# Four graph-attention layers: the four-head output computed transposed, with elu taken from PSUM

## The chip, the cores and the metric

The kernel runs on one core of one Trainium2 chip. The metric is the device time of one execution in microseconds (us), as the median of several runs; lower is better. In profile lines PE is the matrix engine (PEld its weight loads), DVE the vector engine, ACT the scalar engine, POOL the GpSimd engine and SP the queue that issues the transfers.

## What is computed

There are 128 independent graphs of 128 nodes with 512 features. Each passes through four attention layers; after each comes a residual and a layer norm. The change lies in layer 1, which has two attentions in a row. The first has four heads of 256 features:

```python
xl = (x @ W).reshape(B, N, H, F)                       # H = 4, F = 256
e = leaky_relu(asrc[:, :, None, :] + adst[:, None, :, :], 0.2)
attn = softmax(where(mask[..., None], e, -1e9), axis=1)
out = einsum('bsdh,bshf->bdhf', attn, xl).reshape(B, N, H * F) + bias
h = elu(out)                                           # 1024 features
```

Then `h` is multiplied by W2 (1024 to 512 features) and goes through the second attention, of one head. As the weights of one output node sum to one, a bias that is added to every node's features adds the same bias to the output.

## The kernel before

A graph's 128 nodes lie on the 128 partitions, and a graph stays on chip through all layers. All data is float32; each float32 multiply of the matrix engine is two records (two MATMUL with their weight loads) in the profile, a transpose one.

`graph(g)` is a generator that emits one graph's work and stops at each `yield`; we call the part between two yields a step. The outer loop passes over all graphs in flight, oldest first, and lets each emit one step; a new graph joins every 10 passes (`STAGGER`). So in the steady state a pass emits steps r, r+10, r+20 and so on, of graphs that are ten passes apart, and ten passes emit the work of one graph. The tile framework then fixes each engine's queue: it follows the order of emission by priority, but may put a ready instruction ahead of one that waits. Each engine works its queue in order.

`attend` is one softmax: POOL multiplies the identity by the destination scores (`dg`, L160), PE spreads them over the partitions (`pd`, L167), ACT adds the source score (L177), DVE does leaky relu (L181) and adds the mask with a running minimum (L187), ACT takes exp with row sums (L194), DVE inverts the sums (`ri`, L200), PE transposes the weights (`pp`, L203) and DVE copies them to SBUF (`pt`, L206). A graph does this six times: `l0` (one head), `l1` (four), `l2` (one), `l30` and `l31` (four each, the two halves of layer 2's eight heads) and `l4` (one).

The first attention of layer 1 goes so. PE transposes `x1` (L234); `px` (L294) multiplies it by W1 in two halves of 512 columns, of which ACT copies the first to `xl` (L299) and DVE the second (L301). After `attend`, four multiplies `pa` (L311) take the weights `pt` of a head as the stationary operand and 256 columns of `xl` as the moving one. DVE scales by `ri` and adds the bias (L319), takes the minimum with zero (L324), ACT takes exp (L326), DVE forms elu (L328). PE transposes the 1024 features in eight blocks (`h1T`, L234), ACT and DVE copy them (L336, L338), and `pc` (L344, two columns for the scores) and `px` (L352, W2) use them as stationary operands.

PSUM has eight banks of 128 x 512 float32, taken in turn by every `bank()`.

Of the kernel before, what the change touches and what calls it, by code (L numbers as in the profile page):

```python
# [8 lines left out]
F32 = mybir.dt.float32  # L9
I32 = mybir.dt.int32  # L10
AF = mybir.ActivationFunctionType
ALU = mybir.AluOpType
AX = mybir.AxisListType

P = 128
SLOPE = 0.2
EPS = 1e-5
# A masked score is e - BIG, which rounds to -BIG for every e that a score can take.
BIG = float(2.0**100)
FMAX = 3.0e38  # L20
# A graph starts when the one before it has taken this many of its steps.
STAGGER = 10


# [1 line left out]
def tile_gat_stack(  # L26
# [19 lines left out]
    w_attn: bass.AP,  # L46
    out: bass.AP,
):
    """Four graph-attention layers with residual and layer norm. Each graph has 128 nodes, one
    per partition, and passes through all layers on chip; several graphs are in flight."""  # L50
    nc = tc.nc
    B, N, F = x.shape
    H1, FH = a1_src.shape
    HF = H1 * FH
    H2, FO = ah1.shape
    KF = F // P
    KH = HF // P
# [6 lines left out]
    def bank(name):  # L64
        return psum.tile([P, 512], F32, tag="ps", name=name)

# [1 line left out]
    ident = const.tile([P, P], F32, name="ident")  # L68
    make_identity(nc, ident)
    ones = const.tile([P, P], F32, name="ones")  # L70
# [5 lines left out]
    neghalf = const.tile([P, 1], F32, name="neghalf")  # L76
    nc.vector.memset(neghalf, -0.5)

# [1 line left out]
    def rows(ap, n, name, pool=const):  # L80
        t = pool.tile([P, n], F32, name=name)
        nc.scalar.dma_start(out=t, in_=ap.partition_broadcast(P))
# [5 lines left out]
    b1t = rows(b1, HF, "b1t")  # L88
# [6 lines left out]
    for h in range(H2):  # L95
        nc.scalar.dma_start(out=wht[:, :, h, :], in_=wh[h].rearrange("(k p) o -> p k o", p=P))

    # Scores are x @ (W @ a): the products of the weights come first, once.
    wc1 = const.tile([P, KF, 2 * H1], F32, name="wc1")
    wc2 = const.tile([P, KH, 2], F32, name="wc2")  # L100
    wc3 = const.tile([P, KF, 2 * H2], F32, name="wc3")
# [1 line left out]
    with tc.tile_pool(name="setup", bufs=1) as setup:  # L103
        for s, a in enumerate((a1_src, a1_dst)):
            at = rows(a.rearrange("h f -> (h f)"), HF, f"a1_{s}", setup)
            for k in range(KF):
                pr = setup.tile([P, H1, FH], F32, tag="pr1", name=f"pr1_{s}_{k}", bufs=2)
                nc.vector.tensor_mul(pr.rearrange("p h f -> p (h f)"), w1t[:, k, :], at)
                nc.vector.tensor_reduce(
                    out=wc1[:, k, s * H1 : (s + 1) * H1], in_=pr, op=ALU.add, axis=AX.X  # L110
                )
        for s, a in enumerate((a2_src, a2_dst)):
            at = rows(a.rearrange("h f -> (h f)"), F, f"a2_{s}", setup)
            for k in range(KH):
                pr = setup.tile([P, F], F32, tag="pr2", name=f"pr2_{s}_{k}", bufs=2)
                nc.vector.tensor_mul(pr, w2t[:, k, :], at)
                nc.vector.tensor_reduce(out=wc2[:, k, s : s + 1], in_=pr, op=ALU.add, axis=AX.X)
        for s, a in enumerate((ah1, ah2)):
            at = rows(a.rearrange("h f -> (h f)"), F, f"ah_{s}", setup)
            for k in range(KF):  # L120
                pr = setup.tile([P, H2, FO], F32, tag="pr3", name=f"pr3_{s}_{k}", bufs=2)
                nc.vector.tensor_mul(
                    pr.rearrange("p h f -> p (h f)"), wht[:, k].rearrange("p h f -> p (h f)"), at
                )
                nc.vector.tensor_reduce(
                    out=wc3[:, k, s * H2 : (s + 1) * H2], in_=pr, op=ALU.add, axis=AX.X
                )
        fc = setup.tile([OUT, F], F32, name="fc")
        nc.scalar.dma_start(out=fc, in_=w_fc)
        ac = setup.tile([OUT, 2], F32, name="ac")  # L130
        for s in range(2):
            nc.scalar.dma_start(
                out=ac[:, s : s + 1],
                in_=w_attn[0:1, s * OUT : (s + 1) * OUT].rearrange("u o -> o u"),
            )
        for s in range(2):
            # The same column for every output row: the product lands on all partitions.
            acb = setup.tile([OUT, P], F32, name=f"acb_{s}")
            nc.vector.tensor_copy(acb, ac[:, s : s + 1].to_broadcast([OUT, P]))
            pf = bank(f"pf_{s}")  # L140
            nc.tensor.matmul(pf, lhsT=acb, rhs=fc, start=True, stop=True)
            nc.vector.tensor_copy(wf[:, s, :], pf)

    io = ctx.enter_context(tc.tile_pool(name="io", bufs=3))
    wk = ctx.enter_context(tc.tile_pool(name="wk", bufs=3))
# [6 lines left out]
        nc.sync.dma_start(out=at, in_=adj[g])  # L152
        return xt, at

    def attend(g, lay, src, dst, mask, nh, res):
        """softmax over j of lrelu(src[i] + dst[j]) + mask[i, j], as (not normalised, transposed)
        weights [j, h, i] and the inverse of their sums [i, h], for each head."""
        n = f"{lay}_{g}"
        dg = wk.tile([P, 4, P], F32, tag="diag", name=f"dg_{n}")
        nc.gpsimd.tensor_mul(  # L160
# [37 lines left out]
        yield  # L198
        ri = sm.tile([P, 4], F32, tag="ri", name=f"ri_{n}")
        nc.vector.reciprocal(ri[:, :nh], rs[:, :nh])  # L200
        pp = bank(f"pp_{n}")
        for h in range(nh):
            nc.tensor.transpose(pp[:, h * P : (h + 1) * P], z[:, h, :], ident)  # L203
# [6 lines left out]
        res.append((pt, ri))  # L210

    def norm(y, n):
        """(y - mean) / sqrt(var + eps) over the features, in place."""
        st = sm.tile([P, 6], F32, tag="st", name=f"st_{n}")
        nc.vector.bn_stats(st, y)
        mv = sm.tile([P, 2], F32, tag="mv", name=f"mv_{n}")
        nc.vector.bn_aggr(mv, st)
        yield
        rd = sm.tile([P, 1], F32, tag="rd", name=f"rd_{n}")
        nc.gpsimd.tensor_scalar_add(rd, mv[:, 1:2], EPS)  # L220
        nc.gpsimd.tensor_tensor(out=rd, in0=rd, in1=neghalf, op=ALU.pow)  # L221
        yield
        nc.vector.tensor_scalar(  # L223
            out=y, in0=y, scalar1=mv[:, 0:1], scalar2=rd, op0=ALU.subtract, op1=ALU.mult
        )
        yield
# [9 lines left out]

    def graph(g, loaded):
        x0, adj_t = loaded
# [1 line left out]
        m3 = sm.tile([P, P], F32, tag="m3", name=f"m3_{g}", bufs=6)  # L240
        m2 = sm.tile([P, P], F32, tag="m2", name=f"m2_{g}", bufs=6)
        m1 = sm.tile([P, P], F32, tag="m1", name=f"m1_{g}", bufs=6)
# [5 lines left out]
                out=m, in0=a, scalar1=0.0, scalar2=-BIG, op0=op, op1=ALU.mult  # L248
            )

# [1 line left out]
        sc0 = sm.tile([P, 2], F32, tag="sc0", name=f"sc0_{g}")  # L252
        for s, (wv, init) in enumerate(((w0s, b0t), (w0d, 0.0))):
            jk = wk.tile([P, F], F32, tag="junk", name=f"jk0_{g}_{s}", bufs=2)
# [5 lines left out]
        res = []  # L260
# [11 lines left out]
        )  # L272
        yield from norm(x1, f"n0_{g}")

# [1 line left out]
        for xT, pb, _ in transposed(x1, KF, f"x1T_{g}", "xT"):  # L276
            yield
            nc.scalar.copy(xT.rearrange("p k i -> p (k i)"), pb)
# [12 lines left out]
        for c in range(2):  # L291
            px = bank(f"px1_{g}_{c}")
            for k in range(KF):
                nc.tensor.matmul(  # L294
                    px, lhsT=xT[:, k, :], rhs=w1t[:, k, c * 512 : (c + 1) * 512],
                    start=(k == 0), stop=(k == KF - 1),
                )
            if c == 0:
                nc.scalar.copy(xl[:, :512], px)  # L299
            else:  # L300
                nc.vector.tensor_copy(xl[:, 512:], px)  # L301
        yield
        yield from attend(g, "l1", sc1[:, H1:], sc1[:, :H1], m1, H1, res)
        pt, ri = res.pop()
        z1 = wk.tile([P, HF], F32, tag="z1", name=f"z1_{g}", bufs=2)
        t1 = wk.tile([P, HF], F32, tag="t1", name=f"t1_{g}", bufs=2)
        for c in range(2):
            pa = bank(f"pa1_{g}_{c}")
            for u in range(2):
                h = 2 * c + u  # L310
                nc.tensor.matmul(  # L311
                    pa[:, u * FH : (u + 1) * FH], lhsT=pt[:, h, :],
                    rhs=xl[:, h * FH : (h + 1) * FH], start=True, stop=True,
                )
            yield
            for u in range(2):
                h = 2 * c + u
                cols = slice(h * FH, (h + 1) * FH)
                nc.vector.scalar_tensor_tensor(  # L319
                    out=z1[:, cols], in0=pa[:, u * FH : (u + 1) * FH], scalar=ri[:, h : h + 1],  # L320
                    in1=b1t[:, cols], op0=ALU.mult, op1=ALU.add,
                )
        # elu(z) = max(z, exp(min(z, 0)) - 1)
        nc.vector.tensor_scalar_min(t1, z1, 0.0)  # L324
        yield
        nc.scalar.activation(t1, t1, AF.Exp)  # L326
        yield
        nc.vector.scalar_tensor_tensor(  # L328
            out=z1, in0=t1, scalar=-1.0, in1=z1, op0=ALU.add, op1=ALU.max
        )  # L330
        yield
        for hT, pb, c in transposed(z1, KH, f"h1T_{g}", "hT"):
            yield
            dst = hT[:, 4 * c : 4 * c + 4, :].rearrange("p k i -> p (k i)")
            if c == 0:
                nc.scalar.copy(dst, pb)  # L336
            else:
                nc.vector.tensor_copy(dst, pb)  # L338
        yield

# [1 line left out]
        pc = bank(f"pc2_{g}")  # L342
        for k in range(KH):
            nc.tensor.matmul(  # L344
# [21 lines left out]
        )  # L366
        yield from norm(x2, f"n1_{g}")

# [1 line left out]
        for xT, pb, _ in transposed(x2, KF, f"x2T_{g}", "xT"):  # L370
            yield
            nc.scalar.copy(xT.rearrange("p k i -> p (k i)"), pb)
# [38 lines left out]
        nc.vector.tensor_add(x3, x3, x2)  # L411
        yield from norm(x3, f"n2_{g}")

# [1 line left out]
        sc4 = sm.tile([P, 2], F32, tag="sc4", name=f"sc4_{g}")  # L415
        for s in range(2):
            jk = wk.tile([P, F], F32, tag="junk", name=f"jk3_{g}_{s}", bufs=2)
# [21 lines left out]
        yield from norm(y, f"n3_{g}")  # L439
        nc.sync.dma_start(out=out[g], in_=y)  # L440

# [1 line left out]
    loads = {0: load(0)}  # L443
    active, nxt, tick = [], 0, 0
    while active or nxt < B:
# [42 lines left out]
```

## Time and profile before

| | |
|---|---|
| time, median of 3 runs | 4495.4 us (4493.48 to 4498.8) |
| span of the profiled execution | 4494.5 us (its own time is not recorded apart from its span) |
| busy: PE, DVE, ACT, POOL | 97%, 82%, 44%, 37% of the span |
| granted clock of the matrix engine | 0.995 |
| one graph in the steady state | 33.9 us between equal points of two cycles of the chain |

The profile page gives the busy time of each engine, the span in 40 slices, the transfers, and the chain of work that ended last. Two adjoining records of one engine overlap in it, so the spacing of the starts says more about the rate than the duration of a record. The trace behind it gives each instruction with its start, its duration, and what ended the idle time before it.

### The profile page before, as it was taken

The page shows a single profiled execution, that of the slowest core. Times are in us where ns is not written, and L with a number is a line of the kernel's source. Part 1 is how long each engine was busy: PE and PEld are TensorE (multiplying, and loading weights), DVE is VectorE, ACT ScalarE, POOL GpSimd, SP SyncE. Part 2 cuts the span into 40 slices and gives each one's busy share as a digit, 9 for nine tenths or more (in the row PEclk, how much of TensorE's full clock was granted, in tenths as well). Part 3 has the DMA queues.
Part 4 walks back from the last instruction along what each step waited for, and adds up shares of the span by engine and source line. Part 5 has one row for each costly group of instructions (what it writes and reads, how often), then busy time and mean ns, then how long its engine had stood idle before and what let it go on. Part 6 is the DMA issues. An engine that isn't in the chain of part 4 may idle for free.

```text
span 4494.5 us, 61235 instructions
## 1 busy us (share of the span) xinstructions
PE 4348.2 (97%) x18692; PEld 2640.8 (59%) x18692; DVE 3702.8 (82%) x11464; ACT 1968.8 (44%) x6785; POOL 1659.6 (37%) x2438
## 2 busy tenths in 40 slices
PE   1999999999999999999999999999999999999997
PEld 0565666666566666566566666656656656656664
DVE  5688888888888888888888888888888888888887
ACT  0344444444444444444444444444444444444443
POOL 1233333333333333333333333333333333333332
PEclk9999999999999999999999999999999999999998
DMA  2000000000000000000000000000000000000000
GB/s 92 10 17 18 18 19 17 20 19 17 20 19 17 19 20 17 19 20 17 19 17 19 18 19 19 17 20 19 17 19 19 17 19 20 17 19 20 16 10 15
DMA packets 63142, 88.16 MB, mean 20 GB/s; under 512 B 10816, under 2 KB 27200, under 8 KB 62816
## 3 DMA queue, kind: packets, MB, share of 16 engines
q1 hardware_dynamic: 55296, 75.52, 5.1%
q10 hardware_dynamic: 7520, 8.72, 0.6%
q8 instruction: 152, 2.49, 0.2%
q14 instruction: 174, 1.43, 0.1%
HBM read 50.66 MB, written 33.55 MB: 19 GB/s over the span
## 4 chain that ended last, share of the span: by engine, by line
PE 88%; DVE 10%; POOL 1%; ACTq 0%; issue 0%; ACT 0%; DMA 0%; POOLq 0%; SPq 0%; DVEq 0%
PE px L352 20%; PE px L294 20%; PE px L384 10%; PE pd_l L167 9%; PE pa L400 5%; PE pa L311 5%; PE pc L344 4%; DVE z_l L181 4%; PE pp_l L203 3%; PE pa L426 3%; PE pc L284 2%; PE pc L376 2%; DVE pt_l L206 2%; DVE z_l L187 2%; PE x1T_p L234 1%; PE x2T_p L234 1%
## 5 line engine op out<-in xcount | busy, mean ns | idle before, releaser
L160 POOL TENSOR_TENSOR dg_l<-ident,sc 128x128 f32<-128x128 f32 (+1 forms) x768 | 648.6, 845 | 1246.7 <-PE pa L311 585.5
L352 PE MATMUL px<-w2t,h1T 128*128 128x512 f32 x2048 | 941.7, 603 | 0.0
L194 ACT ACTIVATE z_l<-z_l,nm_l 128x128 f32<-128x128 f32 x1920 | 757.8, 414 | 413.3 <-DVE nm_l L187 413.1
L294 PE MATMUL px<-w1t,x1T 128*128 128x512 f32 x2048 | 913.5, 599 | 0.0
L177 ACT ACTIVATE z_l<-pd_l,sc 128x128 f32<-128x128 f32 x1920 | 565.5, 375 | 483.6 <-PE pd_l L167 408.3
L294 PEld LDWEIGHTS px<-w1t,x1T 128*128 128x128 f32 x2048 | 380.5, 191 | 430.5 <-issue 430.2
L352 PEld LDWEIGHTS px<-w2t,h1T 128*128 128x128 f32 x2048 | 369.7, 190 | 367.8 <-issue 367.8
L187 DVE CUSTOM_DVE_ANT_0 z_l<-z_l,m 128x128 f32<-128x128 f32 x1920 | 567.3, 337 | 8.8
L356 ACT COPY xl<-px 128x512 f32<-128x512 f32 x128 | 75.0, 586 | 1068.1 <-PE px L352 1068.1
L167 PE MATMUL pd_l<-dg_l,ones 128*128 128x512 f32 (+1 forms) x1536 | 515.8, 435 | 15.3 <-POOL dg_l L160 15.2
L223 DVE TENSOR_SCALAR x<-x,mv_n,rd_n 128x512 f32<-128x512 f32 x384 | 294.1, 766 | 277.1 <-POOL rd_n L221 277.1
L181 DVE SCALAR_TENSOR_TENSOR z_l<-z_l 128x128 f32<-128x128 f32 (+1 forms) x768 | 504.3, 657 | 8.3 <-ACT z_l L177 8.3
L384 PE MATMUL px<-wht,x2T 128*128 128x512 f32 x1024 | 471.0, 603 | 0.0
L247 POOL TENSOR_SCALAR m<-adj 128x128 f32<-128x128 int32 x256 | 256.0, 1000 | 560.3 <-DVE nm_l L187 549.3
L206 DVE COPY pt_l<-pp_l 128x128 f32<-128x128 f32 (+1 forms) x768 | 369.7, 481 | 90.0 <-PE pp_l L203 89.9
L194 ACT ACTIVATION_READ_ACCUMULATOR z_l<-z_l,nm_l 128x1 f32 x1920 | 399.6, 208 | 0.0
L203 PE MATMUL pp_l<-ident,z_l 128*128 128x128 f32 x1920 | 341.8, 275 | 13.0 <-ACT z_l L194 12.6
L400 PEld LDWEIGHTS pa<-xl,pt_l 128*128 128x128 f32 x2048 | 259.2, 192 | 151.0 <-DVE pt_l L206 91.7
L203 PEld LDWEIGHTS pp_l<-ident,z_l 128*128 128x128 f32 x1920 | 240.4, 145 | 180.3 <-issue 129.6
L221 POOL TENSOR_TENSOR rd_n<-rd_n,neghalf 128x1 f32<-128x1 f32 x512 | 306.9, 599 | 32.5
L167 PEld LDWEIGHTS pd_l<-dg_l,ones 128*128 128x128 f32 x1536 | 243.1, 192 | 124.7 <-issue 98.6
L301 DVE COPY xl<-px 128x512 f32<-128x512 f32 x128 | 88.6, 692 | 269.6 <-PE px L294 269.6
(83 smaller groups left out, 6694.3 us busy)
## 6 DMA issues: line engine op xcount, KB each, us to landing
x<-in_x_dram SPq DMA_DIRECT2D x128, 256.0 KB, 2.6
out_dram<-y SPq DMA_DIRECT2D x128, 256.0 KB, 2.0
adj<-in_adj_dram SPq DMA_DIRECT2D x128, 64.0 KB, 1.7
w1t<-in_L_gnn_W_dram ACTq DMA_DIRECT2D x1, 2048.0 KB, 10.9
w2t<-in_L_gnn_W_dram ACTq DMA_DIRECT2D x1, 2048.0 KB, 16.0
wht<-in_L_gnn_W_dram ACTq DMA_DIRECT2D x8, 128.0 KB, 5.4
b1t<-in_L_gnn_b_dram ACTq DMA_DIRECT2D x1, 512.0 KB, 6.1
a<-in_L_gnn_att_src_dram ACTq DMA_DIRECT2D x1, 512.0 KB, 4.3
```

What stands on the lines that cost most here:

```text
L160: nc.gpsimd.tensor_mul(dg[:, :nh, :], ident.unsqueeze(1).to_broadcast([P, nh, P]), dst.unsqueeze(2).to_broadcast([P, nh, P]),)
L167: nc.tensor.matmul(pd[:, : nh * P], lhsT=ones, rhs=dg[:, :nh, :].rearrange("p h j -> p (h j)"), start=True, stop=True,)
L177: nc.scalar.activation(z[:, h, :], pd[:, h * P : (h + 1) * P], AF.Identity, bias=src[:, h : h + 1])
L181: nc.vector.scalar_tensor_tensor(out=z[:, :nh, :], in0=z[:, :nh, :], scalar=SLOPE, in1=z[:, :nh, :], op0=ALU.mult, op1=ALU.max,)
L187: nc.vector.tensor_tensor_reduce(out=z[:, h, :], in0=z[:, h, :], in1=mask, scale=-1.0, scalar=FMAX, op0=ALU.add, op1=ALU.min, accum_out=nm ...
L194: nc.scalar.activation(z[:, h, :], z[:, h, :], AF.Exp, bias=nm[:, h : h + 1], scale=-1.0, accum_out=rs[:, h : h + 1],)
L203: nc.tensor.transpose(pp[:, h * P : (h + 1) * P], z[:, h, :], ident)
L206: nc.vector.tensor_copy(pt[:, :nh, :].rearrange("p h i -> p (h i)"), pp[:, : nh * P])
L294: nc.tensor.matmul(px, lhsT=xT[:, k, :], rhs=w1t[:, k, c * 512 : (c + 1) * 512], start=(k == 0), stop=(k == KF - 1),)
L352: nc.tensor.matmul(px, lhsT=hT[:, k, :], rhs=w2t[:, k, :], start=(k == 0), stop=(k == KH - 1))
L384: nc.tensor.matmul(px, lhsT=xT[:, k, :], rhs=wht[:, k].rearrange("p h o -> p (h o)"), start=(k == 0), stop=(k == KF - 1),)
L400: nc.tensor.matmul(pa[:, u * FO : (u + 1) * FO], lhsT=pt[:, u, :], rhs=xl3[:, h * FO : (h + 1) * FO], start=True, stop=True,)
```

## The change

In the first attention of layer 1 the output is computed with features on the partitions. Both halves of `px` are now taken out of PSUM by DVE with an addition of the bias. `attend` gets `scaled=True`: POOL multiplies the four heads' weights by the inverse sums before they are transposed, with a yield of its own behind it. The output multiplies take 128 columns of `xl` as the stationary operand and the transposed weights as the moving one: eight of 128 columns in place of four of 256. ACT reads each PSUM bank twice, with exp and with relu, and DVE forms min(exp(z) - 1, relu(z)) straight into `hT`. The eight transposes, the two copies behind them, the scaling out of PSUM and the minimum with zero go. Comments were removed too. From here on steps and lines are those of the kernel before, unless said otherwise.

```diff
-    def attend(g, lay, src, dst, mask, nh, res):
+    def attend(g, lay, src, dst, mask, nh, res, scaled=False):
...
         nc.vector.reciprocal(ri[:, :nh], rs[:, :nh])
+        if scaled:
+            nc.gpsimd.tensor_mul(
+                z[:, :nh, :], z[:, :nh, :], ri[:, :nh].unsqueeze(2).to_broadcast([P, nh, P])
+            )
+            yield
         pp = bank(f"pp_{n}")
...
-            if c == 0:
-                nc.scalar.copy(xl[:, :512], px)
-            else:
-                nc.vector.tensor_copy(xl[:, 512:], px)
-        yield
-        yield from attend(g, "l1", sc1[:, H1:], sc1[:, :H1], m1, H1, res)
+            cols = slice(c * 512, (c + 1) * 512)
+            nc.vector.tensor_add(xl[:, cols], px, b1t[:, cols])
+        yield
+        yield from attend(g, "l1", sc1[:, H1:], sc1[:, :H1], m1, H1, res, scaled=True)
         pt, ri = res.pop()
-        z1 = wk.tile([P, HF], F32, tag="z1", name=f"z1_{g}", bufs=2)
-        t1 = wk.tile([P, HF], F32, tag="t1", name=f"t1_{g}", bufs=2)
+        e1 = wk.tile([P, KH, P], F32, tag="e1", name=f"e1_{g}", bufs=2)
+        r1 = wk.tile([P, KH, P], F32, tag="r1", name=f"r1_{g}", bufs=2)
+        hT = wk.tile([P, KH, P], F32, tag="hT", name=f"hT_{g}", bufs=2)
         for c in range(2):
             pa = bank(f"pa1_{g}_{c}")
-            for u in range(2):
-                h = 2 * c + u
+            for u in range(4):
+                k = 4 * c + u
                 nc.tensor.matmul(
-                    pa[:, u * FH : (u + 1) * FH], lhsT=pt[:, h, :],
-                    rhs=xl[:, h * FH : (h + 1) * FH], start=True, stop=True,
+                    pa[:, u * P : (u + 1) * P], lhsT=xl[:, k * P : (k + 1) * P],
+                    rhs=pt[:, k * P // FH, :], start=True, stop=True,
                 )
             yield
-            for u in range(2):
-                h = 2 * c + u
-                cols = slice(h * FH, (h + 1) * FH)
-                nc.vector.scalar_tensor_tensor(
-                    out=z1[:, cols], in0=pa[:, u * FH : (u + 1) * FH], scalar=ri[:, h : h + 1],
-                    in1=b1t[:, cols], op0=ALU.mult, op1=ALU.add,
-                )
-        # elu(z) = max(z, exp(min(z, 0)) - 1)
-        nc.vector.tensor_scalar_min(t1, z1, 0.0)
-        yield
-        nc.scalar.activation(t1, t1, AF.Exp)
-        yield
-        nc.vector.scalar_tensor_tensor(
-            out=z1, in0=t1, scalar=-1.0, in1=z1, op0=ALU.add, op1=ALU.max
-        )
-        yield
-        for hT, pb, c in transposed(z1, KH, f"h1T_{g}", "hT"):
-            yield
-            dst = hT[:, 4 * c : 4 * c + 4, :].rearrange("p k i -> p (k i)")
-            if c == 0:
-                nc.scalar.copy(dst, pb)
-            else:
-                nc.vector.tensor_copy(dst, pb)
+            cols = slice(4 * c, 4 * c + 4)
+            nc.scalar.activation(e1[:, cols, :].rearrange("p k i -> p (k i)"), pa, AF.Exp)
+            nc.scalar.activation(r1[:, cols, :].rearrange("p k i -> p (k i)"), pa, AF.Relu)
+            yield
+            nc.vector.scalar_tensor_tensor(
+                out=hT[:, cols, :], in0=e1[:, cols, :], scalar=-1.0, in1=r1[:, cols, :],
+                op0=ALU.add, op1=ALU.min,
+            )
         yield
```

## The prediction

> **What bounds the kernel now.** First the page: engine totals and slices.
>
> ```profile
> PE 4348.2 (97%) x18692; PEld 2640.8 (59%) x18692; DVE 3702.8 (82%) x11464; ACT 1968.8 (44%) x6785; POOL 1659.6 (37%) x2438
> PE   1999999999999999999999999999999999999997
> DVE  5688888888888888888888888888888888888887
> PE 88%; DVE 10%; POOL 1%; ACTq 0%; issue 0%; ACT 0%; DMA 0%; POOLq 0%; SPq 0%; DVEq 0%
> ```
>
> PE is busy in every slice behind the start, and the last line, the shares of the chain that ended last, gives PE 88%. But 10% of it is DVE, so I read one cycle of the chain in order of time.
>
> ```profile
> 2002.70 0.79 PE pc L284 x8
> ...
> 2012.51 0.12 PE pp_l L203
> ...
> 2012.66 0.29 DVE pt_l L206
> 2012.95 0.62 DVE z_l L181
> ...
> 2014.53 0.86 DVE z_l L181
> 2015.39 0.61 DVE pt_l L206
> ...
> 2016.04 1.10 PE pa L400 x8
> ...
> 2027.54 0.84 PE pa L400 x8
> 2028.38 0.44 PE x2T_p L234 x4
> 2028.83 0.22 PE pd_l L167 x2
> 2029.05 0.87 PE pa L311 x4
> ...
> 2036.62 0.79 PE pc L284 x8
> ```
>
> A cycle (one graph) is 2036.62 - 2002.70 = 33.92 us. All is PE except 2012.66 to 2016.0, where the chain goes through DVE. What PE does meanwhile stands in its timeline:
>
> ```profile
> 2012.46 0.60 PE L234 MATMUL h1T_p<-ident,z 128*128 128x128 f32 x4
> 2012.89 0.60 PE L203 MATMUL pp_l<-ident,z_l 128*128 128x128 f32 x4
> 2013.33 1.02 PE L361 MATMUL pa<-xl,pt_l 128*128 128x512 f32 x2
> 2014.19 0.60 PE L234 MATMUL h1T_p<-ident,z 128*128 128x128 f32 x4
> ...
> 2015.60 0.27 PE L203 MATMUL pp_l<-ident,z_l 128*128 128x128 f32 x1
> 2016.04 1.10 PE L400 MATMUL pa<-xl,pt_l 128*128 128x64 f32 x8 [0.17 <-DVE pt_l L206]
> ```
>
> PE works there too, from 2012.51 to 2015.71 (2015.60 and one transpose of 0.11), then has nothing until 2016.04: 0.33 us lost. The L400 group then takes 0.94 to the next start (2016.98) where it takes 0.84 at 2027.54: 0.10 more. The stall is 0.43 a cycle; the other 33.49 is PE work without a gap. So PE's queue is the bound, with one joint where DVE sets the pace, and both groups of `h1T` transposes lie exactly at that joint.
>
> **PE, part by part, per graph.**
> Removed: eight `h1T` transposes at 0.44 per four (the x2T piece): -0.88.
> The output multiplies: before, eight records of 256 columns at 0.87 per four: 1.74. After, sixteen records of 128 columns, each with new weights. Columns alone give 0.87/4/2 = 0.109 each, as much per graph as before. Nearest rows: `pd_l` of 128 columns, 0.22 for two, 0.11 each; transposes, 0.44 for four, 0.11 each, also with new weights every time; L284, 8 columns, 0.79 for eight, 0.099, so a weight load alone costs about that and lies under the multiply. Ends: 16 x 0.107 = 1.71 (-0.03) and the stalled L400 group, 1.10 for eight, 0.1375 each, 2.20 (+0.46). I take 0.115 each, 1.84 (+0.10), near to the 0.11 rows.
> The Trainium skill, "TensorE: Matmul & The Clock Gate", section "Back-to-back issue gap", speaks against the split: in a stream of weight loads and multiplies the spacing is set by both, so narrower moving operands pay. Here 0.11 at 128 columns is what columns alone give; if load and stream added (0.099 + 0.107), the sixteen would cost 3.3, +1.6, and the change would lose.
>
> **The joint.** The saved 0.88 lies inside the window that DVE ends. If the joint stayed as it is, PE would come 0.88 earlier to L400 and wait 0.88 longer. Whether it stays is a matter of the order of emission. I counted yields: 79 steps before, 77 after (three fewer for elu and copies, one more for scaling), so everything behind comes two steps earlier against layers 0 and 1 of younger graphs. The DVE work of the window is `pt` of `l0`, leaky relu and mask of `l30` (0.62 and four at about 0.21), leaky relu of `l1` (0.86), and only then `pt` of `l31` (0.61), which L400 waits for. The leaky relu of `l30` falls there because its `pd` (step 46) is emitted two passes behind the 7 us `px` of L294 (step 14). After, it is step 44: same pass, older graph, ahead of that `px`. Its ACT and DVE work can run under the 7 us. The `pp` of `l31` moves from step 58 to 56 and its `pt` to 57, ahead of the leaky relu of `l1` (step 18). Between that `pp` and L400 PE then has L361 0.86, `pd` of `l1` 0.86 and two transposes 0.22: 1.94 for DVE to make one copy of 0.61. So the stall mostly goes: I take -0.30 of the 0.43, ends 0 and -0.43 for the forecast, +0.88 as a rival.
> What is late next: `pc` L344 needs the second elu half. Behind its multiplies stand ACT 0.63 and 0.59 (128x512 rows of L433 and L356) and DVE 0.69 (L435): 1.9 us. PE has 1.94 as above, then L400 0.84, `pp` of `l30` 0.44 and the first half of `pc` 0.79: 4.0. Covered by 2.1. The `pp` of `l1` waits for the new POOL step: ACT 4 x 0.375, DVE 0.76 + 4 x 0.42 (L187 with its accumulator read), ACT 4 x 0.62, DVE 0.16, POOL 1.29 make 7.9 us; in that time PE has two transposes, L400 and `pp` of `l30` (1.5), `pc` L344 (1.6), L352 (7.1), then `pm`, L266, L426, L400, x2T and `pd` of `l2` (3.3): 13.5. Covered by 5.6.
>
> **The other engines.** DVE, page means: out go L301 0.69, L319 4 x 0.48, L324 0.68, L328 1.20, L338 0.68: 5.17. In come two additions from PSUM (nearest L364, 0.74) and two elu halves (L435, 0.69): 2.86. Net -2.3 of some 28.4. The POOL multiply is like the 128x512 `dg` (1.29), and such a one holds DVE back: L181 at 128x128 took 1.13 us at 2033.83 while `dg` ran, and 0.29 at 2011.12 with no such POOL work beside it. Ends 0 and 1.29; I take 0.85 by that row, so DVE is at 27.0 and hides it in PE's 32.8.
> The skill, "SBUF — State Buffer", section "Who interferes with whom", says that the loser of the shared port blocks for the whole instruction; by it the price is up to 1.29, DVE at 27.4, still under PE.
> ACT: out 0.59 + 1.06 + 0.64, in four at 0.59 to 0.63: +0.15 of 15. Relu is new; the trace has one table load (1.28 us) in all for Identity, Copy and Exp. Ends 0 and four loads a graph, 5.1 us, ACT at 20; I take 0. POOL +1.29 on 13. Two PSUM banks fewer are taken per graph, so bank turns can only come free sooner. No transfer moves.
>
> **Sum.** 33.92 - 0.88 + 0.10 - 0.30 = 32.84, -1.08 a cycle. Times 127 cycles: -137. Fill and drain (4494.5 - 127 x 33.92 = 187 us, setup included) I leave alone. Span 4494.5 - 137 = 4357.5; the median lies 0.9 over the span: 4358.
>
> **Rivals.**
> Stall kept or multiplies dear: the mechanism as above, but the joint keeps 0.43 (33.14, 4396) or the multiplies cost +0.46 (33.20 with the stall reduced, 4404). Against the second speak the 0.11 rows. 4380 to 4440.
> The gain ends in the joint: the queues keep the window's DVE order, PE waits 0.88 more, 33.92, no change, 4495. For it: the chain's DVE 10%, and that queues follow emission only loosely. Against it: step numbers above and 2.3 us less DVE work.
> Slower: DVE's queue held behind `px` of L294. Both halves now leave through DVE, so a queue that has the second addition ahead of other work waits for the multiply's end; before, L301 already waited 269.6 us in all. Then up to L400 follow addition 0.69, norm 0.52, `pt` of `l2` 0.28, elu half 0.69, leaky relu and mask of `l4` 0.89 and `l30` 1.64, reciprocals 0.45, `pt` of `l31` 0.68: 5.84. PE has the second half of the output multiplies 0.87, `pp` of `l31` 0.44 and the 1.94: 3.25. Stall 2.6, cycle 32.72 + 2.6 = 35.3, 4671. It costs time from 33.92 - 32.72 = 1.2 of stall, 4.45 us of DVE work behind the multiply. Against it: while L301 waited, DVE had already run the score products (L255) of a younger graph, so ready work is put ahead.
> A change that does nothing is excluded: the transposes are gone from the program.
>
> **How the numbers follow.** Forecast 0.65 (4325 to 4380: stall gone and columns alone give 32.58, 4325; stall half kept 4370). Kept stall or dear multiplies 0.17. Gain eaten 0.09, a third of it within 0.2% (9 us, what a measurement of this kernel can tell from no change), a third each side. Slower 0.09. Faster 0.65 + 0.17 + 0.03 = 0.85, same 0.03, slower 0.12. Range 4322 to 4460: about 0.04 below, 0.15 above.
>
> **What the profile after would show.** A cycle of 32.6 to 33.2 in the chain, DVE's share of the chain down to a few per cent; sixteen output-multiply records per graph at 0.11 between starts; no L400 wait on `pt`; DVE near 81% of the span; one table load. I am wrong if the output multiplies stand 0.13 or more apart, if PE waits at L400, L344 or the `pp` of `l1` for over half a microsecond a cycle, or if DVE idles behind the additions while PE then waits for it.

## The result and the profile after

The changed kernel takes 4675.7 us (median of 4 runs, 4670.2 to 4681.7), the kernel before beside it 4496.9: a ratio of 1.040 (95% interval 1.038 to 1.041), 179 us slower. The forecast was 4358, range 4322 to 4460.

First the page of the changed kernel: engine totals, granted clock and chain.

```profile
span 4668.5 us, 61210 instructions
PE 4325.3 (93%) x18692; PEld 2605.1 (56%) x18692; DVE 3559.1 (76%) x10952; ACT 1928.9 (41%) x6913; POOL 1725.1 (37%) x2566
PE 43%; DVE 41%; POOL 7%; issue 5%; ACT 3%; ACTq 0%; DMA 0%; POOLq 0%; SPq 0%; DVEq 0%
```

PE's share of the chain that ended last fell from 88% to 43%, although DVE is less busy than before (76%). PE's busy share fell too: it waits. The granted clock over the span is 0.977, from 0.995. One joint of the chain in order of time shows both (start, length, work):

```profile
2081.06 0.68 DVE L181 SCALAR_TENSOR_TENSOR z_l<-z_l 128x512 f32<-128x512 f32 x1
2082.27 0.28 DVE L187 CUSTOM_DVE_ANT_0 z_l<-z_l,m 128x128 f32<-128x128 f32 x1
...
2082.59 0.40 ACT L194 ACTIVATE z_l<-z_l,nm_l 128x128 f32<-128x128 f32 x1 [2.35 <-DVE nm_l L187]
2082.90 0.18 ACT L194 ACTIVATION_READ_ACCUMULATOR z_l<-z_l,nm_l 128x1 f32 x1
2082.99 0.56 ACT L381 COPY xl<-px 128x512 f32<-128x512 f32 x1
2083.45 0.58 ACT L283 COPY x1T<-x1T_p 128x512 f32<-128x512 f32 x1
...
2084.09 1.06 PE L289 MATMUL pc<-wc,x1T 128*128 128x8 f32 x8 [1.80 <-ACT x1T L283]
```

These are rows of the DVE, ACT and PE timelines of one cycle. PE's last work before it was one transpose at 2082.02, so it stands still from 2082.13 to 2084.09: 1.96 us, for ACT's copy of `x1T`, transposed already at 2079.38. ACT is not busy with it: it idles 2.35 us, because its queue holds the exp of the first head of `l31` ahead of the copies, and that exp waits for DVE's mask. DVE is late. One reason is in the POOL timeline:

```profile
2069.09 0.23 POOL L225 TENSOR_SCALAR rd_n<-mv_n 128x1 f32<-128x1 f32 x1 [3.01 <-DVE ri_l L200]
2069.27 1.04 POOL L202 TENSOR_TENSOR z_l<-z_l,ri_l 128x512 f32<-128x512 f32 x1
2070.27 0.57 POOL L226 TENSOR_TENSOR rd_n<-rd_n,neghalf 128x1 f32<-128x1 f32 x1
```

The new scaling (L202) lies in POOL's queue between the two small halves of a norm's reciprocal root (L225, L226), and DVE idles 1.82 us for that root (its L228 at 2070.88) ahead of a long stretch, with one more idle of 0.69 us for the next root at 2077.59, that ends at the mask for the exp.

Second, the starts of the L289 group over the chain, with what follows them:

```profile
2012.93 1.06 PE pc L289 x8
2013.99 8.66 PE px L299 x16
...
2049.36 1.06 PE pc L289 x8
2050.41 6.97 PE px L299 x16
2057.38 0.89 PE pa L318 x8
...
2084.09 1.06 PE pc L289 x8
```

A cycle is 2084.09 - 2049.36 = 34.73 us, but the one from 2012.93 is 36.43: the same sixteen multiplies took 8.66 instead of 6.97. Counted over the middle of the run, 39 of 109 cycles are of the long kind, and the mean is 35.34. Before, all of 114 cycles were 33.7 to 34.0 long. The granted clock, asked for two stretches of the slow multiplies and one of the fast ones (columns: stretch, length, busy time of PE, PEld, DVE, ACT, POOL, then the clock, then share and GB/s of the transfers), says what happens:

```profile
2014.20:2017.40 3.20, 3.20 (x6) 1.33 (x5) 3.20 (x12) 3.12 (x14) 2.02 (x2) 0.63 0.24 87
2019.00:2022.00 3.00, 3.00 (x8) 1.33 (x7) 0.83 (x3) 0.32 (x2) 1.10 (x2) 1.00 0.04 11
2050.50:2057.00 6.50, 6.50 (x16) 2.90 (x16) 5.02 (x23) 4.89 (x22) 3.16 (x4) 1.00 0.14 50
```

For some 3.4 us (2 x 1.69) PE runs at half clock; the trace's own clock records put it at 2015.01 to 2018.42, three quarters of the first row. The Trainium skill, "TensorE: Matmul & The Clock Gate", section "What's actually happening", gives two states, half and full, and a window of about 3.4 us; the 0.63 (a mixture of the two) and the 1.00 here agree.

So two costs were open: the wait (34.73 against the forecast's 32.84) and the slow clock (35.34 against 34.73, 0.6 a cycle, 77 us over 127 cycles).

### The profile page after: what moved, and what is told of

Its sections match the earlier page's. It is cut to its first block, busy times and chain, and to the rows that moved or that the text cites. A ratio compares the mean times of both kernels' runs of the same rounds, so it can differ in the third digit from the quotient of the medians.

```text
span 4668.5 us, 61210 instructions
## 1 busy us (share of the span) xinstructions
PE 4325.3 (93%) x18692; PEld 2605.1 (56%) x18692; DVE 3559.1 (76%) x10952; ACT 1928.9 (41%) x6913; POOL 1725.1 (37%) x2566
## 4 chain that ended last, share of the span: by engine, by line
PE 43%; DVE 41%; POOL 7%; issue 5%; ACT 3%; ACTq 0%; DMA 0%; POOLq 0%; SPq 0%; DVEq 0%
PE px L299 21%; DVE z_l L187 7%; PE pc L336 5%; DVE x L228 4%; DVE z_l L181 4%; DVE y L427 4%; DVE st_n L220 3%; DVE pt_l L211 3%; PE pp_l L208 3%; POOL rd_n L226 3%; PE pc L289 3%; POOL z_l L202 3%; PE pa L318 3%; PE pd_l L167 2%; PE pa L392 2%
## 5 line engine op out<-in xcount | busy, mean ns | idle before, releaser
L299 PE MATMUL px<-w1t,x1T 128*128 128x512 f32 x2048 | 985.4, 638 | 0.0
L344 PE MATMUL px<-w2t,hT 128*128 128x512 f32 x2048 | 919.7, 602 | 0.0
L225 POOL TENSOR_SCALAR rd_n<-mv_n 128x1 f32<-128x1 f32 x512 | 116.1, 227 | 1735.4 <-DVE mv_n L222 1360.5
L187 DVE CUSTOM_DVE_ANT_0 z_l<-z_l,m 128x128 f32<-128x128 f32 x1920 | 673.9, 384 | 4.6
L344 PEld LDWEIGHTS px<-w2t,hT 128*128 128x128 f32 x2048 | 382.1, 192 | 432.6 <-issue 432.6
L167 PE MATMUL pd_l<-dg_l,ones 128*128 128x128 f32 (+1 forms) x1536 | 523.4, 436 | 14.8 <-POOL dg_l L160 14.8
L228 DVE TENSOR_SCALAR x<-x,mv_n,rd_n 128x512 f32<-128x512 f32 x384 | 209.1, 545 | 320.4 <-POOL rd_n L226 320.4
L305 DVE TENSOR_TENSOR xl<-px,b1t 128x512 f32<-128x512 f32 x256 | 176.5, 689 | 291.5 <-PE px L299 291.5
L289 PE MATMUL pc<-wc,x1T 128*128 128x8 f32 x1024 | 136.9, 260 | 210.5 <-ACT x1T L283 210.0
L324 ACT ACTIVATE e<-pa 128x512 f32<-128x512 f32 x256 | 153.1, 598 | 412.4 <-PE pa L318 412.4
L226 POOL TENSOR_TENSOR rd_n<-rd_n,neghalf 128x1 f32<-128x1 f32 x512 | 291.7, 570 | 32.5
```

What stands on the lines that cost most here:

```text
L167: nc.tensor.matmul(pd[:, : nh * P], lhsT=ones, rhs=dg[:, :nh, :].rearrange("p h j -> p (h j)"), start=True, stop=True,)
L187: nc.vector.tensor_tensor_reduce(out=z[:, h, :], in0=z[:, h, :], in1=mask, scale=-1.0, scalar=FMAX, op0=ALU.add, op1=ALU.min, accum_out=nm ...
L299: nc.tensor.matmul(px, lhsT=xT[:, k, :], rhs=w1t[:, k, c * 512 : (c + 1) * 512], start=(k == 0), stop=(k == KF - 1),)
L344: nc.tensor.matmul(px, lhsT=hT[:, k, :], rhs=w2t[:, k, :], start=(k == 0), stop=(k == KH - 1))
```

## The experiments

Theory O: the order of ACT's queue, which comes from the two steps that fell away, is the wait. Rivals: S, POOL's scaling; D, the second addition on DVE. All four kernels of the first round ran beside the kernel before (4497.0).

**e1: two empty steps added.** The changed kernel, step numbers behind elu put back.

```diff
                 op0=ALU.add, op1=ALU.min,
             )
         yield
+        yield
+        yield
```

> The changed kernel with two empty steps added behind elu, so that the later layers stand against the younger graphs as they did before (79 steps). No work is added or taken. Theory O (order): the two steps that fell away put the copy of x1T on ACT behind the exp of l31, which waits for DVE, and PE pays 1.96 us a cycle at the multiply of L289 and a slower px one cycle in three. Then this version has no such wait, the granted clock is back at 0.995, a cycle is 32.7 to 33.3 us, the time 4340 to 4420. Theory S (the POOL scaling delays the norm and with it DVE): the same work in the same chain, 4640 to 4680. Theory D (both additions now wait on DVE for px): also 4640 to 4680.

Measured: 4415.9 us, ratio 0.982 (0.981 to 0.984). PE has no wait at L289 any more, and a fast cycle is 32.67 us. But 35 of 117 cycles are 34.4 long and the clock is 0.979. O is right about the wait; that the clock would come back with it was wrong.

**e2: the old arithmetic on the new steps.**

```diff
         nc.vector.reciprocal(ri[:, :nh], rs[:, :nh])
+        if lay == "l1":
+            yield
...
         nc.scalar.activation(t1, t1, AF.Exp)
-        yield
         nc.vector.scalar_tensor_tensor(
             out=z1, in0=t1, scalar=-1.0, in1=z1, op0=ALU.add, op1=ALU.max
         )
-        yield
...
                 nc.vector.tensor_copy(dst, pb)
-        yield
```

> The kernel before with its own arithmetic, but with the step numbers of the changed one: a yield added ahead of the transposes of l1, three taken out around exp, elu and the last copy (77 steps). Theory O: the wait at L289 and the slower clock come without any of the new operations; the eight transposes are still there, so 4650 to 4850. Theories S and D: within 0.7% of the kernel before, 4465 to 4530, since neither POOL scaling nor second addition is in it.

Measured: 4527.8 us, ratio 1.007 (1.006 to 1.009): O missed, and the number fits S and D. Yet the trace is none of the three. The exp is ahead of the copy on ACT here too, but PE does not wait: a fast cycle is 33.58 us, faster than before. The loss is slow clock alone, 35 of 114 cycles of 35.3, clock 0.979. So the queue position does not make the wait by itself: how late DVE is, and what PE still has to do meanwhile, count as well.

**e3: no scaling on POOL.** The weights of the first attention of layer 1 stay unnormalised.

```diff
         if scaled:
-            nc.gpsimd.tensor_mul(
-                z[:, :nh, :], z[:, :nh, :], ri[:, :nh].unsqueeze(2).to_broadcast([P, nh, P])
-            )
             yield
```

> The changed kernel without POOL's multiply of l1's weights (they stay unnormalised there), its yield kept. Theory S: POOL's 1.04 us lies between the two halves of the norm's reciprocal root, which DVE waits for; DVE's long stretch starts 1.0 us earlier, the PE wait falls from 1.96 to below 1.0 and the clock comes back: 4480 to 4540. Theory O: the copy of x1T stays behind the exp of l31, the wait stays above 1 us unless DVE gets ahead by as much: 4520 to 4670. Theory D: no change, 4640 to 4680.

Measured: 4530.9 us, ratio 1.008 (1.006 to 1.009). In one cycle of three or so a wait is left, as this row of its PE timeline:

```profile
2053.45 1.06 PE L286 MATMUL pc<-wc,x1T 128*128 128x8 f32 x8 [0.77 <-ACT x1T L280]
```

0.77 in place of 1.80: in such a cycle the 1.04 of the multiply comes back whole. Over the middle of the run 40 cycles of 113 have this wait and full clock (33.6 us); the other 73 have one fall to half clock in W2's `px`, which costs more than the wait and leaves none (34.4 us). So the clock falls further, to 0.964. S is right as the second ingredient, with its size; its hope for the clock was wrong.

**e4: the first half of `px` copied by ACT, its bias left out.**

```diff
-            nc.vector.tensor_add(xl[:, cols], px, b1t[:, cols])
+            if c == 0:
+                nc.scalar.copy(xl[:, cols], px)
+            else:
+                nc.vector.tensor_add(xl[:, cols], px, b1t[:, cols])
```

> The changed kernel with the first half of px copied by ACT as before, without the bias on those 512 columns. Theory D: DVE no longer waits for that half, the time falls by half the loss or more, below 4590. Theories O and S: DVE idles for px under PE's own work, 4630 to 4690.

Measured: 4678.1 us, ratio 1.040 (1.038 to 1.042), and the same wait of 1.80 at L289. D is out, and with it the "slower" rival of the prediction, whose 4671 lay near the result by chance.

Now the clock. e2 has it without any wait of PE. What differs from the kernel before stands around the scores of the second attention, first in a PE timeline of the kernel before and then in the chain of e1:

```profile
2017.43 0.95 PE L344 MATMUL pc<-wc,h1T 128*128 128x2 f32 x8
2018.24 1.10 PE L352 MATMUL px<-w2t,h1T 128*128 128x512 f32 x2
2019.18 0.95 PE L344 MATMUL pc<-wc,h1T 128*128 128x2 f32 x8
```

```profile
2013.73 0.86 PE pa L271 x2
2014.59 0.11 PE pp_l L208
2014.70 0.84 PE pa L394 x8
2015.54 0.22 PE pp_l L208 x2
2015.77 1.68 PE pc L338 x16
2017.45 1.80 PE px L346 x2
```

Before, the second half of `h1T` was ready late, and the queue put one W2 multiply (two records) between the two groups of eight. In e1 all sixteen follow on: from 2014.59 to 2017.45 PE streams only transposes, 64-column and 2-column multiplies, and the W2 multiplies behind them start slowly (1.80 for two records of 512 columns, where the two of L271 take 0.86). Theory L: such a thin stretch brings the half clock. Rivals: P, a denser load; W, a wait of PE.

**e5: e1 with the two kinds mixed.** **e7: e2 with the same edit.**

```diff
         pc = bank(f"pc2_{g}")
+        px = bank(f"px2_{g}")
         for k in range(KH):
             nc.tensor.matmul(
                 pc[:, :2], lhsT=hT[:, k, :], rhs=wc2[:, k, :],
                 start=(k == 0), stop=(k == KH - 1),
             )
-        sc2 = sm.tile([P, 2], F32, tag="sc2", name=f"sc2_{g}")
-        nc.vector.tensor_copy(sc2, pc[:, :2])
-        px = bank(f"px2_{g}")
-        for k in range(KH):
             nc.tensor.matmul(
                 px, lhsT=hT[:, k, :], rhs=w2t[:, k, :], start=(k == 0), stop=(k == KH - 1)
             )
+        sc2 = sm.tile([P, 2], F32, tag="sc2", name=f"sc2_{g}")
+        nc.vector.tensor_copy(sc2, pc[:, :2])
```

> The realigned kernel (e1) with each two-column multiply for the scores of the second attention followed at once by the 512-column multiply of the same block, in place of eight and eight. Same work. In e1 no wait of PE is left, the median cycle is 32.67 us, but some 35 of 117 cycles hold a px of 8.66 us in place of 6.97. Theory L (PE is clocked down after a stretch of some 3 us in which it streams few columns; here pa of 64 columns, transposes and sixteen records of two columns, 2.9 us): no slow px is left, clock 0.99 or more, 4495 - 127 x 1.25 = 4330 to 4350. Theory P (the clock falls because PE is loaded more densely): no change or more slow cycles, 4405 to 4440. Theory W (it falls after a wait of PE): no wait is there, so nothing changes either.

> The kernel before on 77 steps (e2) with the two-column multiplies mixed in the same way. e2 had a median cycle of 33.58 us and 35 of 114 cycles of 35.2. Theory L: all at 33.6, clock 0.99 or more, 4445 to 4465, faster than the kernel before, as the 0.43 us stall at its joint is gone on 77 steps. Theories P and W: 4515 to 4540 as e2.

Measured beside 4494.5: e5 4357.3 us, ratio 0.969 (0.968 to 0.971), e7 4453.5, ratio 0.990 (0.989 to 0.992). Every one of 119 and 116 cycles is 32.7 and 33.5; the clocks are 0.992 and 0.994. e5 lies 7 us above its range, e7 within. PE is denser than in e1 and e2 and not slower, so P is out.

**e6: the changed kernel, scores of `l1` mixed into the first half of `px` (W1).** The wait stays, the thin work behind it goes; the copy of the scores moves behind that half of `px`.

```diff
-        for k in range(KF):
-            nc.tensor.matmul(
-                pc[:, : 2 * H1], lhsT=xT[:, k, :], rhs=wc1[:, k, :],
-                start=(k == 0), stop=(k == KF - 1),
-            )
...
             for k in range(KF):
+                if c == 0:
+                    nc.tensor.matmul(
+                        pc[:, : 2 * H1], lhsT=xT[:, k, :], rhs=wc1[:, k, :],
+                        start=(k == 0), stop=(k == KF - 1),
+                    )
```

> The changed kernel with the eight-column multiplies for l1's scores mixed into the first half of px (W1), so that PE's wait is followed by 512 columns at once; the wait itself stays. Theory L: the thin stretch is cut from 3.0 to 2.1 us, most slow px of L299 go, the wait of 1.8 us stays: cycle near 34.7, 4590 to 4620. If instead the wait alone brings the slow clock (W): 4650 to 4690.

Measured: 4672.7 us, ratio 1.039 (1.038 to 1.041), 38 of 110 cycles long, as in the changed kernel. L missed here and W's figure was met: a wait of 1.96 with a transpose ahead of it and one 8-column multiply (0.24) behind is enough. As e1 and e2 have slow clock without a wait, neither theory is the whole: a wait counts like thin work.

**e8: one order fixed on ACT.** The changed kernel; the exp of `l31` is queued behind the copy of `x1T` (an order, no wait).

```diff
-            nc.scalar.copy(xT.rearrange("p k i -> p (k i)"), pb)
+            x1copy[0] = nc.scalar.copy(xT.rearrange("p k i -> p (k i)"), pb).ins
...
+        with tc.issue_after(x1copy[0]) if lay == "l31" else nullcontext():
             for h in range(nh):
                 nc.scalar.activation(
                     z[:, h, :], z[:, h, :], AF.Exp, bias=nm[:, h : h + 1], scale=-1.0,
```

> The changed kernel, steps and all, with one order fixed on ACT's queue: the exp of l31 goes behind the copy of x1T. Theory O: this queue position is the whole wait at L289; it goes, the median cycle is 32.6 to 33.0 as in e1, and slow px from the thin stretch ahead of px (W2) stay in some cycles: 4390 to 4440. Theory S (POOL's scaling and DVE's late stretch set the pace): the wait moves to the next reader of DVE's results and at most half of the loss against e1 comes back, 4540 to 4680.

Measured: 4409.8 us, ratio 0.981 (0.980 to 0.983). The same joint on PE and ACT:

```profile
2029.87 0.56 ACT L384 COPY xl<-px 128x512 f32<-128x512 f32 x1
2030.33 0.59 ACT L286 COPY x1T<-x1T_p 128x512 f32<-128x512 f32 x1
2031.75 0.27 PE L211 MATMUL pp_l<-ident,z_l 128*128 128x128 f32 x1
2031.86 0.96 PE L292 MATMUL pc<-wc,x1T 128*128 128x8 f32 x8
```

The copy is done at 2030.92, PE comes at 2031.86 and does not stop. One queue position is worth 4675.7 - 4409.8 = 266 us here, wait and the clock behind it together, with POOL's multiply still in place. O is shown, S is not needed for the repair. 33 of 117 cycles stay long, from the thin stretch ahead of W2, as expected.

**e9: the kernel before, W2 held behind all sixteen 2-column records.** No other change.

```diff
-            nc.tensor.matmul(
+            last = nc.tensor.matmul(
                 pc[:, :2], lhsT=hT[:, k, :], rhs=wc2[:, k, :],
                 start=(k == 0), stop=(k == KH - 1),
-            )
+            ).ins
...
-        for k in range(KH):
-            nc.tensor.matmul(
-                px, lhsT=hT[:, k, :], rhs=w2t[:, k, :], start=(k == 0), stop=(k == KH - 1)
-            )
+        with tc.issue_after(last):
+            for k in range(KH):
+                nc.tensor.matmul(
+                    px, lhsT=hT[:, k, :], rhs=w2t[:, k, :], start=(k == 0), stop=(k == KH - 1)
+                )
```

> The kernel before, steps and work unchanged, with one order fixed on PE's queue: the W2 multiplies stay behind all sixteen records of two columns, where the queue had eight, one W2 multiply (two records), eight. No engine gets more to do. Theory L: a thin stretch of about 3 us now stands ahead of W2's multiplies, slow px appear in some cycles and the time rises by 40 to 80 us: 4535 to 4575. Theories P and W (load, or a wait of PE, as the cause of the slow clock): no change, 4490 to 4505.

Measured beside 4496.8: 4546.5 us, ratio 1.011 (1.010 to 1.013), 50 us for the order of eighteen records. Its fast cycle is 33.93 as before, and 21 of 113 are longer, such as this one:

```profile
1971.07 2.00 PE L344 MATMUL pc<-wc,h1T 128*128 128x2 f32 x16
1972.93 8.64 PE L353 MATMUL px<-w2t,h1T 128*128 128x512 f32 x16
```

L holds, with no wait added (the 0.33 us gap of the joint was there before).

**e10: the changed kernel with both repairs**, the edits of e8 and e5.

> The changed kernel on its 77 steps with both repairs: the exp of l31 behind the copy of x1T on ACT (e8) and the two-column multiplies mixed with those of W2 (e5). Theories O and L together: no wait at L289, no slow px, every cycle 32.7 us, 4345 to 4365, as in e5. If the slow clock has another source on 77 steps: 4400 or more.

Measured: 4348.8 us, ratio 0.967 (0.966 to 0.969), all of 119 cycles 32.67 us, clock 0.994. It beats both kernels, and lies 9 us from the forecast, but with two repairs that the change does not have. Its chain is PE again:

```profile
PE 96%; DVE 2%; POOL 1%; ACTq 0%; ACT 0%; issue 0%; DMA 0%; POOLq 0%; SPq 0%; DVEq 0%
```

## Why the prediction was wrong, by its own steps

**The PE terms were right.** Without waits and slow clock a cycle is 32.67 against the forecast 32.84. The output multiplies take 0.89 for eight records (the L318 piece in the chain above), so 1.78 per graph where 1.74 was: +0.04, forecast +0.10. The transposes give 0.88, and the stall of 0.43 goes whole where 0.30 was taken: 33.92 - 0.88 + 0.04 - 0.43 = 32.65. That DVE sets one joint and that the move by two steps frees it held with the old arithmetic too: 33.58 in e2 and, without slow clock, 33.49 in e7, the whole 0.43. As near to like for like as these runs come, the arithmetic of the change is worth e7 against e10 (which has one order on ACT more), 4453.5 - 4348.8 = 105 us.

**The step that failed is "what is late next".** It looked at three readers (L400, `pc` of W2, the `pp` of `l1`), by the order of emission, and left out the fourth that the shift moves: `pc` of L284 on ACT's copy of `x1T`. In the kernel before, the copy started 0.64 us after the first transpose:

```profile
2029.75 0.60 PE L234 MATMUL x1T_p<-ident,x 128*128 128x128 f32 x4
2030.39 0.59 ACT L278 COPY x1T<-x1T_p 128x512 f32<-128x512 f32 x1
```

In the changed kernel it is 4.07 us (2079.38 and 2083.45). On 77 steps the exp of `l31` stands ahead of the copy, in e2 too; why the framework puts it there, presumably because it reckons it ready earlier, was not looked into. The prediction had itself said that queues follow emission only loosely, and charged that to one rival with 0.09 and no loss.

**The POOL multiply was priced as load, not as delay.** "POOL +1.29 on 13" (1.04 in the row above) and 0.85 of DVE time are both hidden; DVE and POOL are indeed not full. Its cost is where it stands: 1.04 us inside a norm's root that DVE waits for (e3: the wait shown falls from 1.80 to 0.77). The rest of the difference to e2, which had the queue order and no wait, I work out and have not tried alone: in e2 the second half of the output multiplies (0.86, L313) still runs between the last transpose and `pc`, where the change has it behind `px`. 1.96 - 1.03 - 0.86 leaves 0.07.

**The clock was taken as given.** The sum has no term for it. Yet the two groups of 2-column records that come to stand together cost 0.5 us a cycle in e1 and e8, and in the changed kernel half clock behind the wait costs 0.6.

In numbers per cycle: 33.93 before; -1.26 by the change's own terms; +2.07 wait and restart (34.74 - 32.67); +0.60 clock; 35.34. The difference of 1.41 to before, times 127, is 179 us, as measured (that it fits to the microsecond is luck: by the mean cycle before, 33.90, it is 183). Of the "wrong if" signs, "PE waits for over half a microsecond a cycle" was the right one, at a reader that was not in its list.

## What to carry to other kernels

When a change removes or adds steps in an interleaved schedule, its own arithmetic is the small part: list every wait of the bottleneck engine, with the queue of the engine that serves it, and ask what else may now stand ahead of the serving instruction. A new operation on an idle engine is priced by what it is queued between, not by the engine's load. And mix multiplies of few columns among wide ones: where the same stationary block serves both, it cost nothing here (a fast cycle is 32.67 us in e1 and 32.68 in e5).

## What was not expected of the hardware

PE falls to half clock for about 3.4 us without standing still: 2.9 us of transposes, 64-column and 2-column multiplies are enough. In e1 the granted clock is 1.00 from 2014.03 to 2017.43, 0.50 from 2017.44 to 2020.85 and 1.00 again to 2024.27; such an event costs 1.69 us and comes in three cycles of ten. The Trainium skill, "TensorE: Matmul & The Clock Gate", section "Why this matters for your kernels", advises against gaps of over some 3 us between bursts of multiplies. Here a gap of 1.96 us among thin work (e6) did it, and thin work with a gap of only 0.33 us (e9), so the measurement goes further than the advice.

Not every thin stretch does it: in e9 21 cycles of 113, in e1 35 of 117. The clock records in the traces say which. In each of the eight traces with slow cycles (the changed kernel, e1 to e4, e6, e8, e9), every fall to half clock between 300 and 4200 us lasts 3.413 us (twice that in three cases of e9), and within a trace all of them begin on one grid of 3.413 us, to 0.01 us. I then counted, from the starts of PE's records at 0.84 ns a column (512 columns in 0.43 us), for which share of each grid window PE streams columns. Of 8820 windows at full clock, all 107 with a share under 36% are followed by half clock, and none over 40%; between the two are 308, of which 214 are. Waiting, transposes and narrow multiplies enter this count alike, which is why e6 and e9 agree, and a thin stretch is caught only when it falls well into one window. Wherever one lays a window of that length in the same part of the run, the share is at least 43% in the kernel before, 68% in e7 and e10 and 72% in e5, none of which has a slow cycle. The count is an estimate fitted to these traces; no run was made to try it.
